# Own rows in squares of 32, turned by VectorE, with the weights in the order 4p+k

## The chip, the cores and the metric

The kernel runs on one core of a Trainium2 chip. The metric is the device time of one execution in microseconds (us), as the median of several runs. A core has TensorE (PE: matrix products and transposes through a product, results in PSUM), VectorE (DVE), ScalarE (ACT), GpSimd (POOL, which here issues the indirect loads, or gathers) and SyncE (SP, which issues all other loads and stores, in program order). 16 DMA engines move the data of all queues.

## The reference, cut to what matters

A graph with N = 6250 nodes, E = 100000 edges sorted by destination, rows of D = 512 floats. Two graph layers stand one behind the other, each a product of a node's own row and a product of the weighted sum over its edges:

```
h    = relu(layernorm(x))
norm = -dinv[src] * dinv[dst]               # dinv = 1/sqrt(degree), 0 without edges
prop(h) = segment_sum(h[src] * norm, dst)
h1   = h @ W1_0 + prop(h) @ W1_1 + b1
h1   = leaky_relu(layernorm(h1) * gamma + beta, 0.01)
out  = x + h1 @ W2_0 + prop(h1) @ W2_1 + b2
```

All of it is in 32-bit floats.

## The kernel before

The nodes are cut into 49 blocks of 128 rows (the last has 106), the edges into 782 chunks of 128. The first stage (to about 130 us) loads x, norms it, writes the table `tab[0]` (rows of 528 floats: h and the node's dinv), counts degrees with 16-bit products and turns the edge numbers.

Then `usual_path` runs each layer over 66 groups of chunks. For one group, `gather_to` has GpSimd gather rows of the layer's table by `src` into `places` (R = 55 places, one chunk each; line 444, one instruction for a chunk; the first 64 chunks of layer one come from x and are normed in place by `look_up`). `choose` builds on DVE the one-hot matrices `sel` (L559, L570); in layer one `scale` multiplies them by the gathered dinv (L604), which waits for the gather. `sums` multiplies them on TensorE (L615), and ACT copies the sum to `agg` (L625).

For each block whose groups are done comes `turn`: it issues the load of the own rows two blocks ahead (`load`, which calls `load_h`, L508; `AHEAD` = 2 buffers), turns the own rows of this block (`own`: four transposes on TensorE, L519, and one ACT copy to SBUF, L521), adds up the group sums of the block (`place`, L645, with one-hot matrices `there` from DVE, L633) and scales them by -dinv while they are copied from PSUM (L698, tile `an`). `first_half` transposes `an` (L705, copied by DVE at L707) and multiplies `hT` by the weights of the own rows; `second` multiplies `aT` by the weights of the sums (both L531), and `finish` adds the biases, and in layer one norms the rows (L662 to L682) and stores them to the table of layer two, `tab[1]` (L679), and to `h_tab` (L684); in layer two it stores the output (L659). The last three blocks (`EARLY`) have their own rows' product made ahead, in `early`.

A product over 512 is four products over 128: tile `hT` holds the own rows transposed, in four slices k with 128 features on the partitions, and the weights lie in SBUF as four slices of 128 rows. Slice k holds the features 128k to 128k+127:

```
nc.sync.dma_start(t, w.rearrange("(k p) d -> p k d", p=P))
```

The order on TensorE, GpSimd and SP is the program's order; that on DVE and ACT is set by a scheduler. Each engine works in order. The layers are joined so: `gather_ahead` (L454) gathers 18 chunks for layer two as soon as all blocks but the last two are stored in `tab[1]`; the rest follows when these are stored too.

At the start of `usual_path` SP issues, in this order, the weights of layer one, the own rows of blocks 0 and 1, and the four vectors of biases and norms, one row each. TensorE spreads these over the partitions (`widen`, L793), after the second group of sums.

Of the kernel before, what the change touches and what calls it, by code (L numbers as in the profile page):

```python
# [8 lines left out]
F32 = mybir.dt.float32  # L9
BF = mybir.dt.bfloat16  # L10
I32 = mybir.dt.int32
AF = mybir.ActivationFunctionType
# [7 lines left out]
P = 128  # L20
# [2 lines left out]
NO_NODE = 16384  # L23
LOADED = 8
Q = 32
NQ = P // Q
STEP = 3
DRIFT = 32
# [14 lines left out]
def gnn_kernel(  # L43
# [33 lines left out]
    nc = tc.nc  # L77
    N, D = x.shape
# [5 lines left out]
    KD = D // P  # L84
# [6 lines left out]
    rows = [min(P, N - i * P) for i in range(NB)]  # L91
# [10 lines left out]
    tab = [dram.tile([n, w], F32, name=f"tab{i}") for i, (n, w) in enumerate(((NB * P, W), (N + 1, D)))]  # L102
    zero_row = (NB - LATE) * P
    assert N < NB * P
    h_tab = dram.tile([N, D], F32, name="h_tab")

    ident = const.tile([P, P], F32, name="ident")
# [5 lines left out]
    ndinv = const.tile([P, NB], F32, name="ndinv")  # L113
# [14 lines left out]
    w_sb = [const.tile([P, KD, D], F32, name=f"w{i}") for i in range(2)]  # L128
# [12 lines left out]
    w_late = places[:, R:, :D].rearrange("p (i k) d -> p i k d", i=2)  # L141
# [19 lines left out]
    for ids, fill, name in ((src, 0, "src_c"), (dst, NO_NODE, "dst_c")):  # L161
        t = ep.tile([P, NG, P], I32, name=name)
# [12 lines left out]
    groups, i = [], 0  # L175
# [18 lines left out]
    def load_rest(k):  # L194
        if k < 3:
            load_x(*groups[6 + k])
        if k == 2:
            nc.sync.dma_start(tab[1][zero_row : zero_row + 1, :], places[P - 1 : P, RE + NB - 1, :D])
        if k == 3:
            for t, w in zip(w_sb, (W1_1, W1_0)):  # L200
                nc.sync.dma_start(t, w.rearrange("(k p) d -> p k d", p=P))
        if k == 4:
            for t, v in ((bias1, b1), (bias2, b2), (gam, gamma), (bet, beta)):
                nc.sync.dma_start(t[0:1], dup(v, 1))
# [18 lines left out]
    with tc.tile_pool(name="turn", bufs=1) as wp, tc.tile_pool(  # L223
        name="turn_ps", bufs=2, space=bass.MemoryType.PSUM
    ) as wps:
        f = wp.tile([P, NG, P], F32, name="f")
# [181 lines left out]
def usual_path(tc, have):  # L408
# [18 lines left out]
    with ExitStack() as es:  # L427
# [77 lines left out]
        def load_h(layer, i, name, bufs):  # L505
            own_h[i] = pool.tile([P, D], F32, name=name, bufs=bufs)
            for lo, hi in parts(rows[i]):
                nc.sync.dma_start(own_h[i][lo:hi], (h_tab if layer else tab[0])[i * P + lo : i * P + hi, :D])  # L508

        def load(layer, i):  # L510
            if i not in EARLY:
                load_h(layer, i, "h", AHEAD)

        def own(layer, i):

            h, r = own_h.pop(i), rows[i]
            ps = psum.tile([P, KD, P], F32, name="hT_ps")
            for kc in range(KD):
                nc.tensor.transpose(ps[:, kc, :r], h[:r, kc * P : (kc + 1) * P], ident[:r, :r])  # L519
            hT = pool.tile([P, KD, P], F32, name="hT", bufs=1)  # L520
            nc.scalar.activation(hT[:, :, :r], ps[:, :, :r], AF.Copy)  # L521
            return hT
# [163 lines left out]
        def turn(layer, i, left=()):  # L686

            r = rows[i]
            if layer == 1 and i not in EARLY:
                load_x(i)  # L690
            if i + AHEAD < NB:
                load(layer, i + AHEAD)
            hT = None if i in EARLY else own(layer, i)
            for k, aT in left:
                second(layer, k, aT)
            place(i, [g for g in inside[i] if i < NB - 1 or g == NS - 1])
            an = pool.tile([P, D], F32, name="an")
            nc.scalar.activation(an[:r], placed.pop(i)[:r], AF.Copy, scale=ndinv[:r, i : i + 1])  # L698
            return hT, an

        def first_half(layer, i, hT, an, between=None):
# [94 lines left out]
        for layer in range(2):  # L796
# [5 lines left out]
            for g in range(NS):  # L802
                gather_to(layer, STEP * unit[g] + R)
                if layer == 0 and g == NS // 2:
                    for k, w in enumerate((W2_1, W2_0)):
                        nc.sync.dma_start(w_late[:, k], w.rearrange("(k p) d -> p k d", p=P))
                if layer == 0:
                    look_up("hT_ps")
                    find("hT_ps")
# [76 lines left out]
def general_path(tc, x, src, dst, bias1, bias2, gam, bet, w_sb, w_late, dinv, ndinv, ident, iota_r, eps,  # L886
# [37 lines left out]
    w_sb = list(w_sb)  # L924
    for k, w in enumerate(w_late):
        w_sb.append(const.tile([P, KD, D], F32, name=f"w_late{k}"))
        nc.sync.dma_start(w_sb[-1], w.rearrange("(k p) d -> p k d", p=P))
    acc = const.tile([P, NB * D], F32, name="acc")
    dl = const.tile([P, NG * P], F32, name="dl_g")
    sidx = const.tile([P, NG * P], I32, name="sidx_g")  # L930
# [107 lines left out]
    def products(pool, psum, h, r, i, wz, wu, table, add):  # L1038

        hT_ps = psum.tile([P, KD, P], F32, name="hT_ps")  # L1040
        for kc in range(KD):
            nc.tensor.transpose(hT_ps[:, kc, :r], h[:r, kc * P : (kc + 1) * P], ident[:r, :r])
        hT = pool.tile([P, KD, P], F32, name="hT")
        nc.scalar.activation(hT[:, :, :r], hT_ps[:, :, :r], AF.Copy)
        z_ps = psum.tile([P, D], F32, name="z_ps")
        u_ps = psum.tile([P, D], F32, name="u_ps")
        for ps, w in ((z_ps, wz), (u_ps, wu)):
            for kc in range(KD):
                nc.tensor.matmul(ps[:r], hT[:, kc, :r], w[:, kc, :], start=(kc == 0), stop=(kc == KD - 1))
        z = pool.tile([P, D], F32, name="z")  # L1050
        nc.scalar.activation(z[:r], z_ps[:r], AF.Copy, scale=dinv[:r, i : i + 1])
        nc.sync.dma_start(table[i * P : i * P + r, :], z[:r])
        nc.vector.tensor_add(acc[:r, i * D : (i + 1) * D], u_ps[:r], add)
# [157 lines left out]
```

## Time and profile before

| | us |
|---|---|
| runs of the kernel before | 2057.62 (median), 2055.93 and 2058.0 (lowest and highest of 3) |
| profiled execution, its own time | 2057.13 |
| span of that execution | 2055.2 |
| TensorE busy | 1686.4 |
| GpSimd busy | 1513.0 |
| DVE busy | 701.1 |
| ACT busy | 406.6 |

In a row of the profile stand the source line, the engine, the operation, what it writes and reads, the shapes as partitions x elements, the count, the busy time and the mean time of one; then the idle time of the engine before them and what ended it. "SPq" is the queue of SyncE: its rows are issues of DMAs, not their transfers. In a chain each row is a start, a length and what the chain ran through. "issue" is time in which the engine waited for nothing that the profile shows.

### The profile page before, as it was taken

What the parts mean: (1) busy time and instruction counts of PE and PEld (TensorE: products, weight loads), DVE (VectorE), ACT (ScalarE), POOL (GpSimd) and SP (SyncE); (2) the same over time, 40 slices, a digit from 0 to 9 for tenths busy, and PEclk for the clock granted to TensorE, in tenths of its full rate; (3) what the DMA queues carried; (4) which work ended last, traced back from release to release, by engine and by line L of the source; (5) the groups of instructions that cost most, each with busy time, mean ns of one, the idle gap of its engine ahead of it and who ended that gap; (6) DMA issues with size and microseconds to landing.
All of it is one profiled execution on the core that took longest, in us unless ns stands there. A gap on an engine that the chain in (4) does not pass through costs nothing.

```text
span 2055.2 us, 19878 instructions
## 1 busy us (share of the span) xinstructions
PE 1686.4 (82%) x6814; PEld 675.0 (33%) x6814; DVE 701.1 (34%) x1501; ACT 406.6 (20%) x740; POOL 1513.0 (74%) x1578
## 2 busy tenths in 40 slices
PE   5569997788777778777899888888888888898987
PEld 4444432233222223333333223233322223333332
DVE  7955442334434333543452211122121212121221
ACT  8766221112211111221120100110110111010110
POOL 5757777777777777777767777777777777777774
PEclk9769998899898889889999989999999999999999
DMA  9978888888898888888877887887788888778875
GB/s 360 360 258 237 274 265 255 247 262 263 255 298 249 255 248 263 262 254 255 256 240 236 253 249 245 251 255 246 247 252 250 246 252 255 243 249 255 270 237 158
DMA packets 189415, 527.47 MB, mean 257 GB/s; under 512 B 34550, under 2 KB 36112, under 8 KB 189304
## 3 DMA queue, kind: packets, MB, share of 16 engines
q0 software_dynamic: 125120, 415.98, 67.5%
q1 hardware_dynamic: 64184, 110.12, 14.8%
q8 instruction: 56, 0.92, 0.2%
q14 instruction: 55, 0.45, 0.1%
HBM read 474.31 MB, written 51.66 MB: 256 GB/s over the span
## 4 chain that ended last, share of the span: by engine, by line
PE 47%; DMA 25%; POOL 11%; issue 9%; DVE 5%; ACT 1%; SPq 1%; DVEq 0%; POOLq 0%; ACTq 0%
DMA places<-tab,sidx 19%; PE u_ps L531 19%; PE ps L615 13%; POOL places L444 11%; PE an_ps L645 9%; DMA places<-tab,lidx 5%; PE hT_ps L519 2%; PE hT_ps L705 2%; DVE lo L340 1%; DVE hi L340 1%; SPq L508 1%; PE hT_ps L491 1%; PE hT_ps L586 0%; DVE sel L604 0%; DVE st L665 0%
## 5 line engine op out<-in xcount | busy, mean ns | idle before, releaser
L444 POOL DMA_INDIRECT places<-tab,sidx x1212 | 1148.8, 948 | 386.5 <-issue 271.3
L615 PE MATMUL ps<-places,sel 128*32 128x512 f32 x3128 | 523.6, 680 | 155.8 <-DMA places<-tab,sidx 90.2
L645 PE MATMUL an_ps<-agg,there 128*128 128x512 f32 (+1 forms) x580 | 284.5, 623 | 101.8 <-ACT agg L625 96.8
L444 POOL DMA_INDIRECT places<-tab,lidx x270 | 255.5, 946 | 82.2 <-issue 62.1
L615 PEld LDWEIGHTS ps<-places,sel 128*32 128x32 f32 x3128 | 105.0, 119 | 542.7 <-issue 195.9
L570 DVE TENSOR_TENSOR sel<-dlx,nodes_ps 128x384 f32<-128x384 f32 (+3 forms) x134 | 72.2, 540 | 423.8 <-PE ps L615 423.4
L625 ACT ACTIVATE agg<-ps 128x512 f32<-128x512 f32 (+1 forms) x132 | 78.3, 594 | 573.1 <-PE ps L615 552.7
L531 PE MATMUL u_ps<-w,hT 128*128 128x512 f32 (+1 forms) x392 | 178.5, 599 | 13.0 <-ACT hT L521 13.0
L645 PEld LDWEIGHTS an_ps<-agg,there 128*128 128x128 f32 (+1 forms) x580 | 110.6, 200 | 228.8 <-ACT agg L625 115.0
L531 PE MATMUL u_ps<-places,hT 128*128 128x512 f32 (+1 forms) x392 | 179.1, 600 | 2.2 <-ACT hT L521 2.2
L531 PE MATMUL u_ps<-w,aT 128*128 128x512 f32 (+1 forms) x392 | 176.9, 594 | 1.7 <-DVE aT L707 1.7
L531 PE MATMUL u_ps<-places,aT 128*128 128x512 f32 (+1 forms) x392 | 176.6, 593 | 1.5 <-DVE aT L707 1.5
L604 DVE TENSOR_TENSOR sel<-sel,places 128x384 f32<-128x384 f32 (+11 forms) x73 | 35.1, 484 | 375.5 <-DMA places<-tab,sidx 370.0
L656 DVE TENSOR_TENSOR u_ps<-u_ps,bias 128x512 f32<-128x512 f32 x46 | 32.2, 699 | 288.5 <-PE u_ps L531 288.5
L521 ACT ACTIVATE hT<-hT_ps 128x512 f32<-128x512 f32 (+1 forms) x98 | 58.2, 594 | 284.3 <-PE hT_ps L519 283.7
L633 DVE TENSOR_SCALAR there<-iota_r,node_of 128x128 f32<-128x128 f32 (+1 forms) x290 | 86.9, 303 | 66.4 <-PE an_ps L645 63.5
L698 ACT ACTIVATE an<-an_ps,ndinv 128x512 f32<-128x512 f32 (+1 forms) x98 | 67.1, 684 | 206.7 <-PE an_ps L645 206.5
L236 POOL DMA_INDIRECT places<-in_x_dram,sidx x55 | 79.1, 1438 | 36.8 <-issue 9.1
L668 ACT ACTIVATE sd<-mv,eps 128x1 f32<-128x1 f32 (+1 forms) x49 | 14.4, 294 | 455.4 <-DVE mv L666 455.4
L531 PEld LDWEIGHTS u_ps<-w,aT 128*128 128x128 f32 (+1 forms) x392 | 71.8, 190 | 84.3 <-issue 78.3
L531 PEld LDWEIGHTS u_ps<-places,aT 128*128 128x128 f32 (+1 forms) x392 | 72.1, 190 | 83.1 <-issue 80.4
L531 PEld LDWEIGHTS u_ps<-w,hT 128*128 128x128 f32 (+1 forms) x392 | 71.3, 192 | 85.1 <-issue 71.5
(166 smaller groups left out, 1272.9 us busy)
## 6 DMA issues: line engine op xcount, KB each, us to landing
places<-tab,sidx POOLq DMA_INDIRECT x1212, 3.9
h_tab<-g SPq DMA_DIRECT2D x48, 256.0 KB
xt<-in_x_dram SPq DMA_DIRECT2D x48, 256.0 KB
out_dram<-t SPq DMA_DIRECT2D x48, 256.0 KB
tab<-t SPq DMA_DIRECT2D x47, 256.0 KB
h<-tab SPq DMA_DIRECT2D x46, 256.0 KB
h<-h_tab SPq DMA_DIRECT2D x46, 256.0 KB
tab<-places SPq DMA_DIRECT2D x22, 528.0 KB
```

The costliest lines, as they stand in the source:

```text
L236: nc.gpsimd.indirect_dma_start(out=places[:, t, :D], out_offset=None, in_=x, in_offset=bass.IndirectOffsetOnAxis(ap=sidx[:, t : t + 1], ax ...
L340: nc.vector.tensor_tensor(t, s[:, g * 2 * GJ : (g + 1) * 2 * GJ].rearrange("p (j s) -> p j s", s=2)[:, :, None, :] .to_broadcast([EP, GJ, ...
L444: nc.gpsimd.indirect_dma_start(out=places[:, t % R, :] if own_scale else zr(layer, t), out_offset=None, in_=x if layer == 0 and t < RAW el ...
L519: nc.tensor.transpose(ps[:, kc, :r], h[:r, kc * P : (kc + 1) * P], ident[:r, :r])
L521: nc.scalar.activation(hT[:, :, :r], ps[:, :, :r], AF.Copy)
L531: nc.tensor.matmul(u_ps[:r], hT[:, kc, :r], w[:, kc, :], start=(start and kc == 0), stop=(stop and kc == KD - 1))
L570: nc.vector.tensor_tensor(sel[:, q : q + k, :w, :], of, node[:, q : q + k, None, :].to_broadcast([P, k, w, Q]), op=OP.is_equal)
L615: nc.tensor.matmul(ps[q * Q : (q + 1) * Q, :], sel[:, q, s, :], zr(layer, chunk[q][s]), start=(s == 0), stop=(s == len(chunk[q]) - 1 and ( ...
L625: nc.scalar.activation(agg[g][: n * Q], ps[: n * Q], AF.Copy)
L633: behind[1] = nc.vector.tensor_scalar(t[:m, :r], iota_r[:m, :r], node_of[:m, g : g + 1], -(1.0 + i * P), op0=OP.subtract, op1=OP.is_equal)
L645: nc.tensor.matmul(placed[i][:r], t[:m, :r], agg[g][:m, :], start=(g == inside[i][0]), stop=(g == inside[i][-1]))
L698: nc.scalar.activation(an[:r], placed.pop(i)[:r], AF.Copy, scale=ndinv[:r, i : i + 1])
```

## The change

The own rows of a block that is not in `EARLY` are loaded by four DMAs in place of one. Each takes 128 of the 512 columns and puts them on 32 partitions, so that partition 32c+i holds, for g from 0 to 3, the 128 columns of part c of row 32g+i. One DVE transpose, which turns each square of 32x32 by itself, then gives `hT` in SBUF. For this the features are dealt out differently: slice k holds the features 4p+k, p the partition. All four weight matrices are loaded in this order, and whatever else makes a transposed operand follows it: the transposes of the `EARLY` blocks read every fourth column, and the ACT copy of `an` reads PSUM with a step of four and writes the slices one behind the other. The same is done in the path for other graphs (`general_path`), which does not run here.

```diff
+S = 32
...
             for t, w in zip(w_sb, (W1_1, W1_0)):
-                nc.sync.dma_start(t, w.rearrange("(k p) d -> p k d", p=P))
+                nc.sync.dma_start(t, w.rearrange("(p k) d -> p k d", p=P))
...
         def load(layer, i):
             if i not in EARLY:
-                load_h(layer, i, "h", AHEAD)
+                assert rows[i] == P
+                own_h[i] = pool.tile([P, P // S, P], F32, name="h", bufs=AHEAD)
+                of = h_tab if layer else tab[0]
+                for c in range(P // S):
+                    nc.sync.dma_start(own_h[i][c * S : (c + 1) * S],
+                                      of[i * P : (i + 1) * P, c * P : (c + 1) * P].rearrange("(g i) f -> i g f", i=S))

         def own(layer, i):

             h, r = own_h.pop(i), rows[i]
+            if i not in EARLY:
+                hT = pool.tile([P, KD, P], F32, name="hT", bufs=1)
+                nc.vector.transpose(hT.rearrange("p k (g i) -> p g k i", i=S),
+                                    h.rearrange("p g (j k) -> p g k j", k=KD))
+                return hT
             ps = psum.tile([P, KD, P], F32, name="hT_ps")
             for kc in range(KD):
-                nc.tensor.transpose(ps[:, kc, :r], h[:r, kc * P : (kc + 1) * P], ident[:r, :r])
+                nc.tensor.transpose(ps[:, kc, :r], h[:r, kc:D:KD], ident[:r, :r])
...
             an = pool.tile([P, D], F32, name="an")
-            nc.scalar.activation(an[:r], placed.pop(i)[:r], AF.Copy, scale=ndinv[:r, i : i + 1])
+            nc.scalar.activation(an.rearrange("p (k f) -> p k f", k=KD)[:r],
+                                 placed.pop(i).rearrange("p (f k) -> p k f", k=KD)[:r], AF.Copy, scale=ndinv[:r, i : i + 1])
...
                     for k, w in enumerate((W2_1, W2_0)):
-                        nc.sync.dma_start(w_late[:, k], w.rearrange("(k p) d -> p k d", p=P))
+                        nc.sync.dma_start(w_late[:, k], w.rearrange("(p k) d -> p k d", p=P))
```

More of the change, by code (lines that the diff above doesn't have):

```diff
@@ L926, in general_path @@
         w_sb.append(const.tile([P, KD, D], F32, name=f"w_late{k}"))
-        nc.sync.dma_start(w_sb[-1], w.rearrange("(k p) d -> p k d", p=P))
+        nc.sync.dma_start(w_sb[-1], w.rearrange("(p k) d -> p k d", p=P))
     acc = const.tile([P, NB * D], F32, name="acc")
@@ L1041, in products @@
         for kc in range(KD):
-            nc.tensor.transpose(hT_ps[:, kc, :r], h[:r, kc * P : (kc + 1) * P], ident[:r, :r])
+            nc.tensor.transpose(hT_ps[:, kc, :r], h[:r, kc:D:KD], ident[:r, :r])
         hT = pool.tile([P, KD, P], F32, name="hT")
```

## The prediction

> **What bounds the kernel now.** I read the page first: the engines' totals, the chain of work that ended last, and the costliest groups.
>
> ```profile
> span 2055.2 us, 19878 instructions
> PE 1686.4 (82%) x6814; PEld 675.0 (33%) x6814; DVE 701.1 (34%) x1501; ACT 406.6 (20%) x740; POOL 1513.0 (74%) x1578
> ...
> PE 47%; DMA 25%; POOL 11%; issue 9%; DVE 5%; ACT 1%; SPq 1%; DVEq 0%; POOLq 0%; ACTq 0%
> DMA places<-tab,sidx 19%; PE u_ps L531 19%; PE ps L615 13%; POOL places L444 11%; PE an_ps L645 9%; DMA places<-tab,lidx 5%; PE hT_ps L519 2%; PE hT_ps L705 2%; DVE lo L340 1%; DVE hi L340 1%; SPq L508 1%; PE hT_ps L491 1%; PE hT_ps L586 0%; DVE sel L604 0%; DVE st L665 0%
> ...
> L444 POOL DMA_INDIRECT places<-tab,sidx x1212 | 1148.8, 948 | 386.5 <-issue 271.3
> L444 POOL DMA_INDIRECT places<-tab,lidx x270 | 255.5, 946 | 82.2 <-issue 62.1
> ```
>
> TensorE is the busiest engine and holds 47% of the chain, and the transposes that the change removes (L519) hold 2% of it. Read by shares alone, the change would pay. But GpSimd's row L444 says something else: 1482 gathers (1212 and 270), 948 and 946 ns each, and idle time before them that the profile mostly cannot put down to anyone ("issue"). So the second view is the table of stretches: layer one early, layer one late, layer two.
>
> ```profile
> core 0: us, PE busy (x) PEld busy (x) DVE busy (x) ACT busy (x) POOL busy (x), PEclk, DMA share, GB/s
> ...
> 300.00:400.00 100.00, 80.09 (x322) 30.18 (x320) 34.98 (x78) 16.31 (x30) 75.77 (x80) 0.90 0.85 253
> 600.00:700.00 100.00, 82.58 (x336) 32.74 (x334) 41.33 (x101) 16.19 (x30) 75.64 (x81) 0.90 0.84 255
> 1600.00:1700.00 100.00, 82.51 (x305) 29.64 (x299) 18.02 (x39) 9.92 (x16) 75.63 (x80) 0.95 0.80 248
> ```
>
> POOL's columns are the same in all three: 80 or 81 gathers in 100 us, 1.25 us each, whether TensorE is busy 80, 83 or 83 us, DVE 35 or 18, the DMA engines 0.85 or 0.80. A row of gathers that nothing else moves is the clock of this kernel. 1482 times 1.25 is 1852 us of the 2055. The third view, GpSimd's own timeline, shows the few places where the row is broken.
>
> ```profile
> 140.42 0.95 POOL L444 DMA_INDIRECT places<-tab,sidx  x1 [0.30 <-PE u_ps L793]
> 153.52 0.97 POOL L444 DMA_INDIRECT places<-tab,sidx  x1 [12.15 <-PE ps L615]
> ...
> 1045.71 0.95 POOL L444 DMA_INDIRECT places<-tab,sidx  x1 [0.30 <-issue]
> 1052.23 0.94 POOL L454 DMA_INDIRECT places<-tab,eidx  x1 [5.57 <-DMA tab<-t]
> ...
> 1077.56 0.99 POOL L444 DMA_INDIRECT places<-tab,sidx  x1 [2.80 <-DMA tab<-pre]
> ...
> 2031.74 0.94 POOL L444 DMA_INDIRECT places<-tab,lidx  x1 [0.30 <-issue]
> ```
>
> Four things outside the row can be lengthened or shortened: the wait of 12.15 us before 153.52 (for TensorE's first sums), the 5.57 us at the turn of the layers and the 2.80 us at its end (for rows of the first layer's result to be stored), and the 23.5 us between the start of the last gather and the end of the span. From 153.52 to 1045.71, and from 1077.56 to 2031.74, there is no break of weight: (2031.74 - 1077.56) / 1.25 is 763 periods, the 764 gathers of layer two (all but its first 18). What the change does to engines inside these two stretches has no price until it holds up a gather, and a gather waits for TensorE only when the 55 places (R in the code) are used up, some 69 us behind. So the sum goes by the start, the turn and the end.
>
> **The start.** The fourth view is the chain of waits there.
>
> ```profile
> L508 SPq DMA_DIRECT2D h<-tab x46: 319/320/15649, 114.2 to 987.7; - x46
> ...
> 114.20 15.65 SPq L508
> ...
> 129.91 0.42 SPq L508
> ...
> 130.37 6.04 DMA bias<-in_L_gnn_b_dram
> ...
> 136.46 7.19 PE u_ps L793 x8
> ...
> 151.41 4.12 PE ps L615 x24
> ```
>
> SP is an in-order queue. Behind the loads of own rows of blocks 0 and 1 (L508) stand the four loads of biases and norms; TensorE's widening of these (L793) waits for them, the first sums that free places (L615) come after it on TensorE, and the gather at 153.52 waits for those. Before, two loads stand ahead of the biases; after, eight. SP takes 0.32 us for one (median of 46), 0.42 us at this place, where the column of 4-byte writes ahead of it still drains. Six more: 6 x 0.42 = 2.5 us, with 1.9 as the lower end. All of it is on the path.
>
> ```profile
> 5.00:6.00 1.00, 0.00 (x0) 0.00 (x0) 0.29 (x2) 0.00 (x0) 0.00 (x0) 1.00 1.08 311
> 14.00:16.00 2.00, 1.75 (x16) 0.82 (x16) 1.97 (x3) 1.94 (x7) 1.39 (x3) 1.00 1.04 409
> ...
> q0 software_dynamic: 125120, 415.98, 67.5%
> ```
>
> Then the rows of these eight loads must be moved: the same 512 KB in pieces of 512 B in place of 2 KB. The stretch of 5 to 6 us, mostly loads of 512-byte pieces (edge numbers), moves 311 GB/s with the engines full; 14 to 16, rows of 2 KB, 409. So 1.7 us against 1.3: +0.4. The upper end is the gathers' queue: each DMA engine gets 64 pieces instead of 16, and if each of the 48 more stands behind one gather packet (67.5% of 16 engines' 2055.2 us over 125120 packets: 0.177 us) that is 8.5 us. I take 0.4, since the loads of 2 KB landed within the 6.04 us that the bias took behind them, and keep 8.5 for the range. Start: +2.9 (1.9 to 11).
>
> **In the two long stretches.** 46 blocks of each layer change.
>
> ```profile
> L519 PE MATMUL hT_ps<-ident,h 128*128 128x128 f32 x368 | 61.2, 292 | 0.8 <-DVE xt L479 0.8
> L521 ACT ACTIVATE hT<-hT_ps 128x512 f32<-128x512 f32 x96 | 57.1, 595 | 269.9 <-PE hT_ps L519 269.4 <-ACT agg L625 0.2
> ...
> L657 DVE TENSOR_TENSOR t<-u_ps,xt 128x512 f32<-128x512 f32 x46 | 31.8, 691 | 1.6
> L698 ACT ACTIVATE an<-an_ps,ndinv 128x512 f32<-128x512 f32 x96 | 65.7, 684 | 204.3 <-PE an_ps L645 204.1
> L232 ACT ACTIVATE sidx<-fT 128x128 int32<-128x128 f32 x6 | 1.5, 272 | 5.5 <-PE fT L230 5.5
> ...
> L519 PE MATMUL hT_ps<-ident,pre x24: 253/272/328, 916.1 to 1956.6; 128*128 128x128 f32 x16, 106*128 106x106 f32 x8
> ```
>
> Removed: 4 transposes of 292 ns, 1.17 us of TensorE a block (107 us in 92 blocks), and the copy out of PSUM, 0.59 us of ACT (55 us). Added on DVE: one transpose of 128x512 f32, SBUF to SBUF. The trace has none; its nearest row by size is L657 with 691 ns, and I take 0.69; twice that is the upper end (64 to 127 us over the kernel, on an engine that is 20 to 40% busy). Added on SP: 3 more loads of 0.32 us a block, about 1 us in some 19; behind them wait only stores and loads with a block's time to spare. DMA: 128 rows become 512 pieces; by the two stretches above 0.87 us against 0.64 for a block, 0.2 us in 19, at 0.80 to 0.85 load. All this lies beside the row of gathers and costs nothing; were the cover of 69 us gone, the removed 1.17 would count as a gain and the added 0.69 as a loss. The transposes of the three last blocks stay on TensorE and read every fourth word; the last of them starts at 1956.6 in layer two, ahead of where the end's chain begins, so even doubled they are hidden.
>
> The weights' order makes runs of 8 KB out of 2 KB: 2 MB of the loading stage, nothing or a few tenths gained; I count 0.
>
> **The turn and the end.** Here the chain has no slack.
>
> ```profile
> 1005.86 0.56 DVE sel L604
> ...
> 1022.92 0.44 PE hT_ps L519 x4
> ...
> 1038.71 0.70 ACT an L698
> ...
> 1062.36 0.69 ACT an L698
> ...
> 2002.99 5.47 DMA places<-tab,lidx
> ...
> 2019.62 0.69 ACT an L698
> ...
> 2042.43 0.69 ACT an L698
> ```
>
> At the turn the chain goes from DVE's scaling at 1005.86, through the finish of block 43 or so behind it, to TensorE, which then works on to 1068 almost without a break. In the built program a transpose stands on DVE between that scaling and the finish: +0.69 (to 1.38). TensorE's transposes at 1022.92 go: 0.44 on the chain, 0.59 at most. Net +0.2. ACT's copy L698 now reads PSUM with a step of 16 bytes. It stands on the chain at 1038.71 and 1062.36, and at 2019.62 and 2042.43 at the end. No row has such a read; its own row (0.68) is the lower end, +0; for the upper I let every element cost double: from 128 to 512 elements ACT goes from 272 to 595 ns, 0.84 ns each, so +0.43. Nothing in the trace tells which; I take the middle, 0.2 each, 0.8 for four. The end's chain begins with the gather of 2002.99 and has no own-row transposes in it: nothing to gain.
>
> A page speaks against this change here. The Trainium skill (SBUF — State Buffer, Door 1: The DMA port swizzle) says that SBUF works in lines of 16 bytes and PSUM in lines of 8, and that an access pays when each element falls in a new line; the new DVE read and the new ACT read both do that. By that rule both upper ends hold, and the sum would be 1.6 us higher (0.7 for DVE, 0.9 for ACT). No run here shows it yet.
>
> **Sum.** Start 2.9, turn 0.2, ACT's four 0.8: +3.9 us. The profiled execution took 2057.13 us (its span 2055.2 and 1.9 around it), so 2061.0; the median of the three runs is 2057.62, which gives 2061.5. A difference of 0.2%, 4.1 us, is about what a measurement can tell from no change; the bound is 2061.7, and the forecast lies just on it. Its own range is 2058.5 to 2064.
>
> **Rivals.** (a) The start costs more: the small pieces drain behind the gathers, up to +11 in place of 2.9, so up to 2070. For it: the bias needed 6.04 us for 2 KB, so that queue is slow already. Against: in that stretch only a few gathers are under way. It decides once the bias lands after 141.
>
> (b) The DVE transpose holds up gathers, slower by far. One DVE operation of this kernel does that:
>
> ```profile
> 18.51 3.48 DVE L340 TENSOR_TENSOR hi<-s_hi,iota_g 125x3136 bf16<-125x3136 bf16 x2
> ...
> 18.58 2.53 POOL L236 DMA_INDIRECT places<-in_x_dram,sidx  x1 [0.30 <-issue]
> ```
>
> A gather that starts under L340 takes 2.53 us in place of 0.95. If the transpose did the same, it would cover the start of a gather in 0.69 / 1.25 = 55% of 92 cases, for 0.35 us on average: +18, 2079 with the rest; at twice the length 2061.5 + 92 x 0.69 = 2125. Against: L340 is a 16-bit operation at double rate, and the stretches with DVE 35 and 18 busy have one and the same row of gathers. The Trainium skill (SBUF — State Buffer, SBUF: two separate sides) states the rule: a DVE operation that uses two ports locks GpSimd out. The pair of rows agrees; whether a transpose is one, no row shows.
>
> (c) TensorE was the bound after all: then L519's 2% of the chain, 41 us, come back, about 2018. For it: 47% of the chain and TensorE 80 to 88% busy. Against: equal gathers in every stretch, and hardly a wait of GpSimd for TensorE. It decides if the period falls under 1.25.
>
> (d) The change does not do what it says: the built program has 92 transposes on DVE, 368 loads and no L519 for these blocks, so this is nearly excluded.
>
> **Chances.** Forecast 0.65: of it 0.33 above the bound and 0.32 within. (a) beyond the forecast's range 0.16, (b) 0.06, (c) and other gains, such as a turn that falls better, 0.10, (d) 0.03. So slower 0.33 + 0.16 + 0.06 = 0.55, same 0.32 + 0.03 = 0.35, faster 0.10. The range takes the forecast, most of (a), and the smaller gains: 2056 to 2070. Left out: 2018, and 2079 and above.
>
> **What would show it.** Right: gathers at 1.25 us in both layers; the bias loads issued 2 to 3 us later and the gather of 153.52 at 155.5 to 157; the L444 rows unchanged at 946; the turn's length within 1 us. Right for the parts: DVE's transpose near 0.7, `an` near 0.7 to 1.1, TensorE about 107 us less busy without a gain. Wrong: a period other than 1.25, gathers longer than 946 ns beside transposes, a new break in GpSimd's row, or a start that did not move.

## The result, and the profile after

The changed kernel takes 2063.65 us (median of 7 runs, 2062.47 to 2067.91); beside it the kernel before took 2055.93 (7 runs, 2053.42 to 2058.0). The medians are 7.7 us apart; the ratio, formed over all the runs, is 1.0041, with a 95% interval of 1.0029 to 1.0053. The profiled execution of the changed kernel took 2067.91 us, the longest of its seven, with a span of 2066.1; so the pair of profiles shows 10.9 us, of which some 3 are that one execution's.

The page of the changed kernel (busy time, share and count by engine; the queue of SP's transfers; the chain that ended last; two groups):

```profile
span 2066.1 us, 19565 instructions
...
PE 1658.0 (80%) x6446; PEld 636.9 (31%) x6446; DVE 792.8 (38%) x1593; ACT 353.3 (17%) x648; POOL 1508.4 (73%) x1578
...
q1 hardware_dynamic: 103160, 110.14, 16.4%
...
PE 43%; DMA 28%; POOL 12%; issue 10%; DVE 5%; ACT 1%; DVEq 0%; POOLq 0%; SPq 0%; ACTq 0%
...
L525 DVE STREAM_TRANSPOSE hT<-h 128x512 f32<-128x512 f32 x92 | 100.5, 1093 | 133.5 <-PE u_ps L542 119.8
L709 ACT ACTIVATE an<-an_ps,ndinv 128x512 f32<-128x512 f32 (+1 forms) x98 | 67.1, 684 | 356.6 <-PE an_ps L656 356.4
```

The work moved as the diff says: TensorE and ScalarE do less, VectorE has 92 transposes more. GpSimd's busy time (1508 us, 1513 before) and its share of the chain (12%, 11% before) are nearly the same. The table of stretches shows the same rate as before:

```profile
300.00:400.00 100.00, 80.93 (x313) 30.36 (x311) 40.47 (x85) 13.93 (x26) 75.89 (x80) 0.92 0.89 260
1600.00:1700.00 100.00, 83.08 (x291) 26.74 (x290) 24.76 (x47) 7.45 (x12) 75.62 (x81) 0.93 0.84 250
```

80 and 81 gathers in 100 us. So the time is in the breaks, and GpSimd's timeline is where to look (start, duration, idle time before it and what ended it; the gathers' line is now L445):

```profile
156.86 0.98 POOL L445 DMA_INDIRECT places<-tab,sidx  x1 [10.70 <-PE ps L626]
...
1052.16 0.95 POOL L445 DMA_INDIRECT places<-tab,sidx  x1 [0.30 <-issue]
...
1084.26 0.94 POOL L445 DMA_INDIRECT places<-tab,sidx  x1 [2.88 <-DMA tab<-pre]
...
2039.40 0.95 POOL L445 DMA_INDIRECT places<-tab,lidx  x1 [0.30 <-issue]
```

Set against the four rows of before, the 10.9 us fall apart like this. The first column is when the row resumes after its break at the start; the others are lengths, from these gathers' starts: layer one's row, the turn, layer two's row, and from the last gather's start to the end of the span. The experiments stand below; all kernels of this table ran on chips on which the kernel before takes some 2055 us.

| kernel | resumes | layer one | turn | layer two | end | span |
|---|---|---|---|---|---|---|
| before | 153.52 | 892.19 | 31.85 | 954.18 | 23.46 | 2055.2 |
| after | 156.86 | 895.30 | 32.10 | 955.14 | 26.70 | 2066.1 |
| e1, after once more | 153.56 | 893.88 | 31.92 | 953.95 | 25.39 | 2058.7 |
| e2, after, biases first | 150.90 | 894.34 | 31.04 | 955.77 | 27.45 | 2059.5 |
| e3, weights' order alone | 150.70 | 892.31 | 31.17 | 953.86 | 24.16 | 2052.2 |
| e4, squares, turned by TensorE | 155.14 | 891.92 | 31.99 | 953.91 | 25.94 | 2058.9 |
| e9, every transpose twice | 154.55 | 893.12 | 31.54 | 954.03 | 24.66 | 2057.9 |
| e10, change in layer two alone | 150.65 | 892.80 | 31.13 | 954.49 | 23.53 | 2052.6 |

Pair by pair, the start gives +3.3, layer one +3.1, the turn +0.25, layer two +1.0 and the end +3.2. The table already warns that one pair isn't enough: the same kernel resumed at 156.86 and at 153.56, and two kernels that load whole rows at the start, e3 and e10, at 150.7 where the kernel before did at 153.52.

### The profile page after: what moved, and what is told of

It is laid out like the page before. It is cut to its first block, busy times and chain, and to the rows that moved or that the text cites. A ratio compares the mean times of both kernels' runs of the same rounds, so it can differ in the third digit from the quotient of the medians.

```text
span 2066.1 us, 19565 instructions
## 1 busy us (share of the span) xinstructions
PE 1658.0 (80%) x6446; PEld 636.9 (31%) x6446; DVE 792.8 (38%) x1593; ACT 353.3 (17%) x648; POOL 1508.4 (73%) x1578
## 4 chain that ended last, share of the span: by engine, by line
PE 43%; DMA 28%; POOL 12%; issue 10%; DVE 5%; ACT 1%; DVEq 0%; POOLq 0%; SPq 0%; ACTq 0%
DMA places<-tab,sidx 22%; PE u_ps L542 19%; PE ps L626 11%; POOL places L445 11%; PE an_ps L656 8%; DMA places<-tab,lidx 5%; PE hT_ps L717 2%; DVE hi L341 1%; DMA tab<-dinv 1%; DVE lo L341 1%; PE hT_ps L492 1%; DVE hT L525 1%; PE both_ps L355 1%; DVE st L676 0%; PE hT_ps L597 0%
## 5 line engine op out<-in xcount | busy, mean ns | idle before, releaser
L445 POOL DMA_INDIRECT places<-tab,sidx x1212 | 1152.1, 951 | 388.8 <-issue 266.0
L656 PE MATMUL an_ps<-agg,there 128*128 128x512 f32 (+1 forms) x580 | 297.9, 648 | 124.2 <-ACT agg L636 124.2
L445 POOL DMA_INDIRECT places<-tab,lidx x270 | 255.4, 946 | 83.0 <-issue 59.8
L525 DVE STREAM_TRANSPOSE hT<-h 128x512 f32<-128x512 f32 x92 | 100.5, 1093 | 133.5 <-PE u_ps L542 119.8
L237 POOL DMA_INDIRECT places<-in_x_dram,sidx x55 | 71.4, 1297 | 45.9 <-ACT places L312 9.6
L542 PEld LDWEIGHTS u_ps<-places,hT 128*128 128x128 f32 (+1 forms) x392 | 71.2, 192 | 73.8 <-issue 71.2
```

The costliest lines, as they stand in the source:

```text
L237: nc.gpsimd.indirect_dma_start(out=places[:, t, :D], out_offset=None, in_=x, in_offset=bass.IndirectOffsetOnAxis(ap=sidx[:, t : t + 1], ax ...
L445: nc.gpsimd.indirect_dma_start(out=places[:, t % R, :] if own_scale else zr(layer, t), out_offset=None, in_=x if layer == 0 and t < RAW el ...
L525: nc.vector.transpose(hT.rearrange("p k (g i) -> p g k i", i=S), h.rearrange("p g (j k) -> p g k j", k=KD))
L542: nc.tensor.matmul(u_ps[:r], hT[:, kc, :r], w[:, kc, :], start=(start and kc == 0), stop=(stop and kc == KD - 1))
L656: nc.tensor.matmul(placed[i][:r], t[:m, :r], agg[g][:m, :], start=(g == inside[i][0]), stop=(g == inside[i][-1]))
```

## The experiments

Theory A: the price is paid once, at the start, by the loads ahead of the biases in SP's queue; the rest is chance of one execution. Theory B: the VectorE transposes cost something, through gathers. Theory C: 512-byte pieces cost the DMA engines all along.

**e1 to e4 ran on one chip, beside 29 runs of the kernel before (2055.37 us).** e1 is the changed kernel without an edit.

> The changed kernel as it is, run once more with a new profile: the yardstick of the runs beside it. In the first pair of profiles the row of gathers lost 3.34 us at the start (it resumed at 156.86 in place of 153.52), 3.1 us in layer one, 0.25 at the turn, 0.96 in layer two and 3.24 after the start of the last gather. Theory A (the price is paid once, at the start, by the loads that stand ahead of the biases in SyncE's queue; what came on top in layer one and at the end is chance of one execution): about 2061 to 2064 us, the row resumes near 157 again, and layer one's stretch and the end move by some us from profile to profile. Theory B (the VectorE transposes hold the gathers up): layer one's stretch is near 895 again and layer two's is longer than 954.2. Theory C (512-byte pieces cost the DMA engines): both stretches are longer again.

2061.22 us; ratio 1.0034 (1.0024 to 1.0044). Less than the first time, and the two intervals overlap. Layer two's row is back at 953.95: most of its +1.0 was one idle time of 1.00 us before the gather at 1816.74, for which the profile names no one, and which e1 does not have. The start is shorter too, and not as expected: the row resumes at 153.56, not near 157. Layer one is shorter, but still 1.7 us above the kernel before.

e2 moves four small loads:

```
+        load_rest(4)
         for i in range(AHEAD):
             load(0, i)
-        load_rest(4)
```

> The changed kernel with the loads of the four bias and norm rows issued ahead of the first two blocks' own rows instead of behind them; all else as in the changed kernel. Theory A: the first 1 x 512 product no longer waits for the squares' issues; the row of gathers resumes about 3.3 us sooner than in the changed kernel, at 153.5 or before, and the time falls by 2.5 to 3.5 us against the changed kernel, to within 3 us of the kernel before. Theories B and C: the start is not where the time is; it stays within 1 us of the changed kernel.

2056.98 us; ratio 1.0011 (1.0002 to 1.0020), 0.23% under e1. The row resumes at 150.90, 2.7 us sooner than in e1, and layer one's row stays long (894.34). The start is where most of the time is. But a wait took the place of the one removed. The timelines of e2: SP, TensorE (widening of the biases, L805), VectorE.

```profile
66.53 1.66 SPq L205 DMA_DIRECT2D bias<-in_L_gnn_b_dram  x2
...
123.53 1.12 PE L805 MATMUL u_ps<-bias,ident 1*128 1x512 f32 x2
...
137.25 2.07 PE L805 MATMUL u_ps<-bet,ident 1*128 1x512 f32 x2 [11.74 <-DVE bias L806]
```

```profile
135.54 1.08 DVE L525 STREAM_TRANSPOSE hT<-h 128x512 f32<-128x512 f32 x1 [10.46 <-DMA h<-tab]
136.54 0.65 DVE L806 COPY bias<-u_ps 128x512 f32<-128x512 f32 x1
```

The loads of the first biases are issued at 66.53 us, and TensorE multiplies them at 123.5. It then needs VectorE's copy of the first result (L806), and that copy stands in VectorE's queue behind the first own-row transpose, which waits 10.46 us for its squares. TensorE waits 11.74 us, nearly as long as for the biases before.

e3 is the weights' order alone: whole rows, turned by TensorE, with a step of 16 bytes. Against the kernel before it has these lines:

```
+            nc.tensor.transpose(ps[:, kc, :r], h[:r, kc:D:KD], ident[:r, :r])
...
+            nc.scalar.activation(an.rearrange("p (k f) -> p k f", k=KD)[:r],
+                                 placed.pop(i).rearrange("p (f k) -> p k f", k=KD)[:r], AF.Copy, scale=ndinv[:r, i : i + 1])
...
+                nc.sync.dma_start(t, w.rearrange("(p k) d -> p k d", p=P))
```

> The weights' order 4p+k alone: own rows are loaded whole, as before, and turned by TensorE, which reads them with a step of 16 bytes; ScalarE scales the neighbours' sums with the step of 16 bytes as in the changed kernel. Neither squares nor VectorE transposes. Theories A, B and C: the time of the kernel before within 1 us (2055 to 2058), the row resumes at 153.5. If the order or the strided reads cost something on TensorE or ScalarE, the scaling of an (684 ns) or the transposes of h (590 ns for 4) take longer, and the time is above the kernel before by more than 2 us.

2054.23 us; ratio 0.9997 (0.9988 to 1.0006): nothing. Its groups:

```profile
L520 PE MATMUL hT_ps<-ident,h 128*128 128x128 f32 x368 | 64.2, 299 | 0.8 <-DVE xt L480 0.8
L520 PEld LDWEIGHTS hT_ps<-ident,h 128*128 128x128 f32 x368 | 57.2, 206 | 61.3 <-issue 52.4 <-PE ps L616 7.7 <-DVE xt L480 1.0
L699 ACT ACTIVATE an<-an_ps,ndinv 128x512 f32<-128x512 f32 (+1 forms) x98 | 67.2, 686 | 204.4 <-PE an_ps L646 204.2
```

ScalarE's strided read of PSUM takes 686 ns against 684 before.

e4 is the squares alone: the same four loads, turned by TensorE, weights as in the kernel before, against which the lines stand.

```
+                own_h[i] = pool.tile([P, 4, P], F32, name="h", bufs=AHEAD)
+                for c in range(4):
+                    nc.sync.dma_start(own_h[i][c * 32 : (c + 1) * 32],
+                                      of[i * P : (i + 1) * P, c * P : (c + 1) * P].rearrange("(g i) f -> i g f", i=32))
...
+                nc.tensor.transpose(ps[:, kc, :r], h[:, kc] if i not in EARLY else h[:r, kc * P : (kc + 1) * P],
+                                    ident[:r, :r])
...
+            if i not in EARLY:
+                nc.scalar.activation(hT.rearrange("p k (g i) -> p g k i", i=32),
+                                     ps.rearrange("p g (k i) -> p g k i", i=32), AF.Copy)
```

> The load in squares alone: four DMAs of 512-byte pieces per block, exactly as in the changed kernel, but TensorE turns the squares (four transposes, and a ScalarE copy that puts the columns in order), and the weights lie as before. No VectorE transpose. Theory A: the start's 3.3 us are there (the row resumes near 157), and nothing else; 2058.5 to 2060.5 us. Theory B: the start counts here too, but what remains of the 7.7 us (about 4) is missing. Theory C: all of it is here, 2062 to 2065 us.

2058.84 us; ratio 1.0020 (1.0010 to 1.0030), so 4.1 us (2 to 6). The first product of the biases and the gather that ends the break, of e3 and then of e4:

```profile
133.64 2.07 PE L795 MATMUL u_ps<-bias,ident 1*128 1x512 f32 x2 [9.73 <-DMA bias<-in_L_gnn_b_dram]
...
150.70 0.97 POOL L445 DMA_INDIRECT places<-tab,sidx  x1 [11.29 <-PE ps L616]
```

```profile
138.08 2.07 PE L802 MATMUL u_ps<-bias,ident 1*128 1x512 f32 x2 [14.87 <-DMA bias<-in_L_gnn_b_dram]
...
155.14 0.97 POOL L444 DMA_INDIRECT places<-tab,sidx  x1 [15.61 <-PE ps L624]
```

In both the row resumes 17.06 us after that product. It is 17.06 or 17.07 in before, after, e1, e9 and e10 too: what lies between is fixed, and the whole start hangs on when the first bias lands. With squares that is 4.4 us later here. Both stretches of e4 (891.92 and 953.91) are as before, with all the 512-byte pieces in them: theory C falls.

**e9 and e10 ran on another such chip, beside 18 runs of the kernel before (2054.91 us).** They repeat e5 and e7 (below). e9 makes every transpose twice; the second is the same line again, so it writes the same values and there is no other order of columns, as the expectation has it:

```
                 nc.vector.transpose(hT.rearrange("p k (g i) -> p g k i", i=S),
                                     h.rearrange("p g (j k) -> p g k j", k=KD))
+                nc.vector.transpose(hT.rearrange("p k (g i) -> p g k i", i=S),
+                                    h.rearrange("p g (j k) -> p g k j", k=KD))
```

> The changed kernel with every VectorE transpose made twice (the second overwrites the first's output, and its columns are in another order, so the sums of layers are other ones; the amount of work counts), once more, because the last four runs were on a chip where the kernel before itself takes 2446 us. On a chip where it takes some 2056: theory A (layer one's 2 us were chance) 0 to 1 us above the changed kernel (2059 to 2063 beside a kernel before of 2055.5), layer one's row of gathers 892 to 895 us; theory B1 (the transposes shift VectorE's scalings of sel onto starts of gathers) 1 to 3 us above the changed kernel, layer one's row 895 to 897, layer two's 954; theory B2 (a transpose itself holds gathers up) over 4 us above it, layer two's row longer too.

2061.38 us; ratio 1.0032 (1.0021 to 1.0044), the same as e1's: 100 us more of VectorE cost nothing that can be measured. Layer one's row is 893.12, shorter than the changed kernel's. VectorE's and GpSimd's timelines in layer two:

```profile
1609.33 1.10 DVE L525 STREAM_TRANSPOSE hT<-h 128x512 f32<-128x512 f32 x1 [2.54 <-PE u_ps L544]
1610.46 1.10 DVE L527 STREAM_TRANSPOSE hT<-h 128x512 f32<-128x512 f32 x1
```

```profile
1609.35 0.95 POOL L445 DMA_INDIRECT places<-tab,sidx  x1 [0.30 <-PE u_ps L544]
1610.60 0.95 POOL L445 DMA_INDIRECT places<-tab,sidx  x1 [0.30 <-issue]
```

Two gathers begin while a transpose runs and take 0.95 us as ever. In the whole execution 157 do, and the longest takes 0.98. So no gather that begins under a transpose is held up.

e10 makes the change in layer two only:

```
             if i not in EARLY:
-                assert rows[i] == P
+                if layer == 0:
+                    return load_h(layer, i, "h", AHEAD)
...
-            if i not in EARLY:
+            if i not in EARLY and layer == 1:
```

> The change in layer two alone, once more for the same reason: in layer one own rows are loaded whole and turned by TensorE, in layer two in squares and by VectorE. Theory A and B1 (the change costs some 3.5 us at the start, through the loads ahead of the biases, and B1 some 2 us in layer one): within 1.5 us of the kernel before, the row of gathers resumes where it did without squares (150.7 to 153.5), layer one's row 892 us, layer two's 954. If the end pays (25.4 to 27.5 us after the last gather's start with squares, 23.5 and 24.2 without): 1 to 3 us above the kernel before.

2055.47 us; ratio 1.0003 (0.9994 to 1.0012): nothing, with 46 transposes and 184 loads of squares in it.

```profile
150.65 0.97 POOL L445 DMA_INDIRECT places<-tab,sidx  x1 [11.53 <-PE ps L627]
...
1074.58 0.94 POOL L445 DMA_INDIRECT places<-tab,sidx  x1 [2.25 <-DMA tab<-pre]
...
2029.07 0.95 POOL L445 DMA_INDIRECT places<-tab,lidx  x1 [0.30 <-issue]
```

So the end doesn't pay either: 23.53 us from the last gather to the end, with the change in force there. All of the cost is paid before the turn.

**e5 to e8 ran on a third chip and e11 and e12 on a fourth, on which the kernel before itself takes 2446.40 (35 runs) and 2472.29 us (23 runs).** They can't speak of the 2055 us, and are told for what they are. e5 is e9's kernel, e7 is e10's, e6 and e11 are the kernel before with e2's edit, and e8 and e12 the changed kernel with e2's edit and this one (with the same condition ahead of the VectorE transpose):

```
+                if layer == 0 and i < AHEAD:
+                    return load_h(layer, i, "h", AHEAD)
```

> The changed kernel with every VectorE transpose made twice, the second overwriting the first's output (its output is wrong in the order of some columns, the amount of work is what counts): 92 more of 1.09 us each on VectorE, 100 us in all, nothing else changed. So far: with the order alone or with the squares alone layer one's row of gathers took 892.3 and 891.9 us, as before (892.2); with VectorE transposes 895.3, 893.9 and 894.3, and there were 19 to 22 gathers above 1.0 us in place of 10 to 15. Theory A (chance of one execution): within 1 us of the changed kernel, layer one's row 892 to 895. Theory B1 (the transposes shift VectorE's scalings of sel onto the starts of gathers, 2 us in layer one): as much again or a little less, 1 to 3 us above the changed kernel, layer one's row 895 to 897, layer two's unchanged. Theory B2 (a transpose itself holds gathers up): in both layers, some 4 us or more above the changed kernel.

2428.79 us; ratio 0.9929 (0.9901 to 0.9957).

> The kernel before with the four bias and norm loads ahead of the first two blocks' own rows; nothing of the change in it. In the changed kernel the same edit let the first products of the biases run at 123.5 us instead of 136 to 140, but VectorE's copies of their results then stood behind the first VectorE transpose, which waited 10.5 us for its squares, so that TensorE stood still all the same. Theory D (the start's break of the row, 12.15 us, is TensorE's wait for the biases, and in the changed kernel that of the transpose): without transposes nothing holds VectorE, TensorE goes on at 124 us, and most of the break goes: 8 to 12 us less than the kernel before, 2043.5 to 2047.5. Rival (the break is also set by the gathers from the table, which start at 134 us, or by the clock): 1 to 3 us less, 2052 to 2054.

2444.92 us; ratio 0.9993 (0.9962 to 1.0024).

> The change in layer two alone: in layer one own rows are loaded whole and turned by TensorE (reading with a step of 16 bytes, for the order of the weights), in layer two in squares and by VectorE. Theory A and B1 (what the change costs is paid in layer one: some 3.5 us at the start through the loads, some 2 us by lengthened gathers): within 1.5 us of the kernel before, the row resumes at 150.7 to 153.5, layer one's row at 892. If the end pays (the last stretch was 25.4 to 27.5 us with the change, 23.5 and 24.2 without squares): 1 to 3 us above the kernel before.

2440.06 us; ratio 0.9984 (0.9954 to 1.0014).

> The changed kernel with the biases loaded first, and the first two blocks of layer one loaded whole and turned by TensorE; all other blocks in squares and by VectorE. Theory D: no transpose stands ahead of the copies of the biases on VectorE, TensorE goes on at 124 us and the row's break at the start mostly goes: 7 to 11 us less than the same kernel with squares everywhere (2057), so 2046 to 2050; layer one's 2 us stay. Rival (the break is set by something else): 2055 to 2057, the row resumes at 150 again.

2445.20 us; ratio 1.0002 (0.9978 to 1.0026).

> The kernel before with the four bias and norm loads ahead of the first two blocks' own rows, once more, on a chip where the kernel before takes some 2056 us. Theory D (the break of the row at the start, 11.3 to 12.2 us with whole rows, is TensorE's wait for the biases): TensorE goes on at about 124 us in place of 134 to 136, and most of the break goes: 8 to 12 us less than the kernel before, 2043.5 to 2047.5. Rival (the break is also set by the gathers from the table, which begin at 132 to 134 us, or by the clock): 0 to 3 us less, 2052 to 2056.

2472.02 us; ratio 1.0001 (0.9982 to 1.0020).

> The changed kernel with the biases loaded first and the first two blocks of layer one loaded whole and turned by TensorE; all others in squares and by VectorE. With squares everywhere and the biases first the row resumed at 150.9 us, because VectorE's copies of the biases stood behind a transpose that waited 10.5 us for its squares. Theory D: no transpose stands ahead of those copies, TensorE goes on at 124 us and the break mostly goes: 7 to 11 us less than with squares everywhere (ratio 1.0011 to the kernel before), so 6 to 10 us under the kernel before. Rival: the row resumes near 150.7 again, and the time is that of the kernel before within 2 us.

2479.13 us; ratio 1.0026 (1.0001 to 1.0051).

On these chips the row of gathers alone isn't the clock. e6's page and group:

```profile
PE 1750.0 (72%) x6814; PEld 711.4 (29%) x6814; DVE 701.8 (29%) x1501; ACT 408.6 (17%) x740; POOL 1520.6 (62%) x1578
...
L444 POOL DMA_INDIRECT places<-tab,sidx x1212 | 1153.8, 952 | 611.9 <-issue 318.2
```

A gather takes 952 ns as ever, but 612 us of idle time stand before the 1212 gathers in place of 386.5. The waits of e11, which has the same instructions (engine, line, releaser: us in total, times, longest; for "remote" the view found no releaser):

```profile
POOL places L444 <- remote: 245.6, 93, 6.9
...
POOL places L444 <- PE ps L615: 122.0, 34, 13.3
```

34 stops end with TensorE's sums, which free the places; the 93 others end with the same semaphore, TensorE's, without a product that the view could name. There the change, even with doubled transposes, is 0.7% faster (e5); that fits a TensorE that holds the places, but e8 and e12, with nearly as much taken off TensorE, gain nothing, so it isn't shown. Whether the biases first, without a transpose in their way, beats both kernels (theory D) was not decided: on these two chips it makes no difference to the kernel before, and on the others it wasn't run without the transposes.

## Why the prediction was right, point by point

Slower, by 7.7 us in the medians; the forecast was 2061.5 with a range to 2070, and 2063.65 lies in the forecast's own range. The clock of the kernel, the main place of the loss and its sign were right. The size was partly luck: the sum was +3.9 on 2057.62, the change costs 6 to 8 us, and the kernel before came out lower beside it (2055.93). Of the +3.9 the start's 2.9 was near; ScalarE's 0.8 was nothing, and some 2 us in layer one were missing.

**The row of gathers.** Right: 1.25 us in all stretches, and 28 us less of TensorE (1686.4 to 1658.0) brought nothing. (Layer one's rate is not quite layer two's; see the long stretches.) "About 107 us less busy" was wrong: 4 x 292 ns adds durations of matmuls that overlap. The busy column beside them said 61.2 us for all 368.

**The start.** Forecast +2.9; the pair of profiles shows +3.3. Over all: with squares at the start the row resumes at 155.0 on average (after, e1, e4, e9), with whole rows at 151.6 (before, e3, e10), +3.4. The groups just do not overlap (153.56 is the lowest with squares, 153.52 the highest without). The undoing (e2, e10) and the doing alone (e4) agree. But the sum came out with two terms missing that nearly cancel: a wait and a shorter landing. SP's timeline and the chain of the changed kernel:

```profile
114.67 23.57 SPq L517 DMA_DIRECT2D h<-tab  x8
138.28 0.58 SPq L205 DMA_DIRECT2D bias<-in_L_gnn_b_dram  x2
```

```profile
113.58 24.34 DMA tab<-dinv
...
138.28 1.47 DMA bias<-in_L_gnn_b_dram
139.79 7.19 PE u_ps L805 x8
```

The chain of e1, and its SP queue's own wait there (total, times, longest):

```profile
114.53 18.18 DMA h<-tab
132.73 3.72 DMA bias<-in_L_gnn_b_dram
136.50 7.19 PE u_ps L805 x8
```

```profile
SPq L205 <- DMA h<-tab: 2.1, 2, 1.2
```

In this pair the bias loads are issued 7.9 us later (138.28 against 130.37), in e1, e4 and e9 at 132.73, 133.45 and 134.40. Before the change the chain runs from SP's issues straight to the bias; with squares it runs through the landing of an earlier DMA: of the first square in e1, e4 and e9, of the column of 4-byte writes (`tab<-dinv`) in the changed kernel, whose eighth square waits for it. The semaphores in the traces say why. SP's DMAs use eight semaphores in turn, and each of the loads here waits until the DMA eight before it has landed. With two loads ahead of the biases, that one is a store of the table, and the bias loads wait for nothing; with eight, it is the first square.

So on average the bias is issued 5.3 us later with squares (after, e1, e4, e9) than without (before, e3, e10). In the traces' issue times, 0.8 of it is the first load, which SP holds longer; 2.8 is six more issues, a step of 0.47 us each, so the forecast's 2.5 was near; and 1.6 is mostly the wait for an earlier DMA's landing, which the forecast did not have. On the other side, the bias then lands sooner after its issue (1.5 to 4.6 us with squares, 4.2 to 6.0 without), which takes off 1.9 and leaves 3.4; that the transfers ahead of it have drained in the meantime fits, but was not tested. Moving the small pieces, the forecast's +0.4, is not seen as a term of its own. (Of the forecast's transfer times, a block of 256 KB at 311 GB/s is 0.84 us, not 0.87; nothing rests on it.) Rival (a) called for a landing after 141; the latest of the four came at 139.75.

**The turn.** +0.2 forecast, +0.25 in the pair. With squares it is 31.5 to 32.1 us in four of five, with whole rows 31.1 to 31.9; no more can be said.

**ScalarE's strided read.** 0.2 us each, 0.8 in all, should have been 0: 684 ns before and after. Here the rule of the Trainium skill that the prediction weighed (SBUF — State Buffer, Door 1: The DMA port swizzle; an access pays for each new line) does not agree with the trace for PSUM read by ScalarE.

**The VectorE transpose.** 0.69 us taken, twice that as the upper end; it takes 1.09. Whether the step of 16 bytes makes it so long no run tells. It is hidden, as e9 shows, and rival (b) is out. What lengthens gathers is another VectorE operation. GpSimd and VectorE of the changed kernel in layer one:

```profile
190.35 1.24 POOL L445 DMA_INDIRECT places<-tab,sidx  x1 [0.30 <-DVE ac L501]
```

```profile
190.23 0.55 DVE L615 TENSOR_TENSOR sel<-sel,places 128x384 f32<-128x384 f32 x1
```

The scaling of `sel` reads two tiles of SBUF; the gather that begins under this one takes 1.24 us in place of 0.95. The same happens in the kernel before:

```profile
644.37 1.31 POOL L444 DMA_INDIRECT places<-tab,sidx  x1 [0.30 <-DMA places<-tab,sidx]
```

```profile
644.31 0.56 DVE L604 TENSOR_TENSOR sel<-sel,places 128x384 f32<-128x384 f32 x1 [14.17 <-DMA places<-tab,sidx]
```

There all ten gathers that begin with more than 0.14 us of a scaling still to run end 0.82 us after the scaling does; the ten that begin in its last 0.14 us take 0.94 or 0.95. In the changed kernel it is the same, but for two that begin within 0.03 us of a scaling's start and take 0.94 and 0.95. The Trainium skill (SBUF — State Buffer, SBUF: two separate sides) says that a VectorE operation with two SBUF inputs, beside a GpSimd operation that reads SBUF, takes the port pair that the two share for its whole length. The trace agrees: 1.24 us under the scaling, 0.95 under the transpose, which has one input.

**The long stretches.** Taken as 0. Layer two is: 953.9 to 954.5 in four of the six kernels with squares there, 954.2 and 953.9 without; the other two (after and e2, 955.1 and 955.8) each have one idle time of 1.0 or 1.6 us before a gather, for which the profile names no one. Layer one is not quite: with VectorE transposes in it 893.1 to 895.3 (after, e1, e2, e9), without 891.9 to 892.8 (before, e3, e4, e10), 1.9 us apart on average. The failed step is "what the change does to engines inside these two stretches has no price until it holds up a gather, and a gather waits for TensorE only when the 55 places (R in the code) are used up": a gather can also be made longer.

The traces show that this is the whole of the loss there. The 712 gathers of layer one's row add up to 676.5 to 679.0 us in the first group and 675.6 to 676.3 in the second, 2.0 us apart on average; the idle time between them is not longer (0.2 us less on average). In the first group 15 to 22 of these gathers take over 1.0 us, in the second 10 to 15, most of them begun under a scaling; those begun under one make up 1.3 of the 2.0. The price was in the record before the change: the ten long gathers of the kernel before cost it 2.3 us.

Doubling the transposes didn't double it (893.1), so it is not a price per transpose; that the shifted order on VectorE lets more scalings fall on a gather's beginning is only argued. In the times e1 stands 0.14% above e4, and their intervals overlap.

**The end.** Taken as 0.4, all of it from ScalarE's read, which cost nothing; +3.2 in the pair. The chain of the changed kernel:

```profile
2016.86 1.04 PE ps L626 x2
2017.91 0.95 PE hT_ps L717 x4
2018.86 8.19 PE u_ps L542 x16
```

The same place in the kernel before, and the clock of the changed kernel there (the column behind POOL's):

```profile
2009.55 0.59 PE hT_ps L705 x4
2010.14 6.87 PE u_ps L531 x16
```

```profile
2018.00:2020.00 2.00, 2.00 (x6) 1.33 (x6) 0.69 (x1) 0.60 (x1) 1.55 (x2) 0.50 0.78 231
```

1.7 of the 3.2 us are a stretch of half TensorE clock that falls on the chain here; before, it fell on the last two microseconds, behind all of TensorE's work. e3, with nothing of the squares or the transposes in it, has such a stretch on its last eight products (5.22 us in place of 3.70), and e10, with all of the change in layer two, has none on its chain. The rest of the pair's 3.2 is 0.8 in the transfer of one gather (6.23 us against 5.47, at 2010.59 and 2002.99 on the chains) and 0.8 behind the last product; none of it is a transpose or a load of own rows. What remains at the end is chance between executions as far as these runs show.

So of about 6 to 8 us, the start is shown to be some 3.4 (the places in the profiles) to 4.7 (e1 less e2 in the times). About 2 are gathers made longer in layer one by the kernels that turn squares on VectorE there; e2, without the start's loss, stands 0.11% or 2.3 us above the kernel before. Why more of the gathers are lengthened there, and what makes up the rest where these two fall short of the whole, were not settled.

## What to carry to other kernels

Find the row that sets the time and ask of every edit only where that row is broken: taking work off a busy engine beside it is worth nothing, and adding 100 us to a half idle one costs nothing (28 us of TensorE and e9's second transposes here). In an in-order queue count what stands behind an instruction that will wait, on SP and on the compute engine alike: e2's early biases were held by a transpose that waited for other data. Count also whose landing an issue waits for: six more loads on SP cost 2.8 us as issues, and made the next load wait for a transfer that it had nothing to do with. And profile the same kernel twice before explaining the third microsecond.

## What was not expected of the hardware

- The first SP load behind a column of 4-byte writes held SP for 13.2 to 16.8 us in all eight kernels of the table; most of the loads behind it took 0.42 to 0.48 us each, as a load of a square does in the whole of the changed kernel (median 0.43).
- A gather that begins under the scaling of `sel` (VectorE, two SBUF inputs, 0.56 us) with more than 0.14 us of it still to run ended 0.82 us after the scaling, ten times out of ten in the kernel before, and took up to 1.31 us in place of 0.95.
- VectorE's transpose of 128x512 f32 in 32x32 blocks, read with a step of 16 bytes, takes 1093 ns, and begins beside gathers without harm to either.
- TensorE's weight load of a 128x128 f32 tile read with a step of 16 bytes takes 206 ns in e3, and 149 without the step in the kernel before (means of 368); it doesn't show in the time.
- The same program takes 2055 us on some chips and 2446 or 2472 on others, with equal gathers and 0.85 of TensorE's clock granted in place of 0.91. The cause is not in these traces.
